# A Hyena block with routed experts on one core: half a forward transform, and work moved between VectorE, ScalarE and GpSimd

## The chip, the cores and the metric

The kernel runs on one core of a Trainium2 chip. The metric is the device time of one execution in microseconds; the median of the runs counts. The engines are TensorE (PE; PEld is its weight load), VectorE (DVE), ScalarE (ACT), GpSimd (POOL) and SyncE (SP, which issues most DMAs). Everything is computed in float32.

## The reference

Eight sequences of 512 tokens with 256 channels pass a long-convolution mixer and a layer of experts, each with a residual and a layer norm without gain (`_layernorm`).

```python
def mixer(x):                                  # x: 8 x 512 x 256
    u = x @ W_in + b_in                        # 768 channels
    uc = short_conv(u, short_w, short_b)       # three taps along the tokens
    x0, x1, v = split(uc, 3)
    v = v * x1
    k = gen_filter(512, ...)                   # 512 x 256, a small net of sines times a decay
    v = causal_fft_conv(v, k, filter_bias)     # product of spectra of length 1024
    return (v * x0) @ W_out + b_out

def ffn(x):                                    # 4096 tokens
    probs = softmax(x @ gate_w.T)              # 16 experts
    top_w, top_idx = top_k(probs, 4)
    top_w = top_w / sum(top_w)
    routed = sum over the 4 of top_w * (silu(x @ w1.T) * (x @ w3.T)) @ w2.T
    shared = (silu(x @ sw1.T) * (x @ sw3.T)) @ sw2.T
    return routed + shared

x = layernorm(x + mixer(x))
x = layernorm(x + ffn(x))
```

## The kernel before

**Mixer, once for each sequence b.** `front` multiplies the transposed input with W_in on TensorE: six products `u_ps` (m = 0 and 1 are the gate x0, 2 and 3 are x1, 4 and 5 are v), 128 channels by 512 tokens each, L409. `convolve_short` does the three taps: ACT writes u + bias and the scaled middle tap (L392, L393), DVE adds the two lagged taps in place (L398). `gated_v` multiplies v by x1. TensorE transposes v in four blocks of 128 tokens (`vt_ps`, L451), ACT evicts (L427), and `transform` (L472) does the forward transform: four outputs (cosine and sine part, two halves of 128 frequencies), each two matmuls of 128x512. ACT evicts each into `vf`. `product` multiplies `vf` with the filter's spectrum on DVE (L488 to L502) into `pf`; `convolved` transforms back (`y_ps`, L522); `gated_y` adds the filter bias and multiplies with the gate x0 on DVE (L538); `normed` multiplies with W_out (`z_ps`, L594). `residual` adds b_out to the input tile `xn` on DVE (L579); `add_z` adds z_ps (L614) and takes the mean and variance with batch-norm statistics on DVE (L554, L555). `scaled` takes the square root on ACT (L562), the reciprocal on DVE and normalizes on ACT (L570) into `x1`. `filter_transform` makes the filter's spectrum once, with the same `transform`.

**Routing.** `turned` transposes x1; `router` computes the gate logits (`l_ps`, L640), picks four experts and their weights on DVE and stores weight and return address beside each token in `x1`. `route` ranks the tokens of each expert with five matmuls (`r_ps`, L780 and L782: one for totals, four with a lag to sum over the four token groups q) and DVE turns ranks into row numbers (`at`). `scatter` sends each token's row four times to the experts' lists `xs` in DRAM, in 16 indirect DMAs on POOL (L925). `shared` computes the shared expert; its sum with x1 goes to DRAM (`kept`).

**Experts.** The sequences form two sets, 0 to 5 and 6 to 7; `listed` makes lists of tiles of 128 rows, 111 tiles for the first set (in three batches) and 47 for the second. `fetch` loads four tiles and DVE picks out each row's weight `sel` and return address `to` (L1061 to L1068). `expert_pair` takes two tiles at a time: transposes (`xr_ps`, L1098), ACT copy, first layer (`h_ps`, L1112), silu on ACT (L1123), product on DVE (L1126), transposes (L1132), ACT copy (L1137), second layer (`o_ps`, L1144), then the eviction with the row weight, on ACT (two halves, L1155) or on DVE (L1157), whichever the planner thinks is free. Two indirect DMAs on POOL (L1166) send the rows back to `results`, by token. `returned` loads the results of a set when its last is sent; `add_up` adds the four of each token (L1199, L1201) with statistics as above, and `finished` normalizes and writes out.

**Order.** All engines are in order, and the order is fixed when the program is built: `Plan` simulates jobs. Each job yields turns (engine, cost, needs, buffers, rank); the planner takes for each engine the lowest rank among those that can start about now. `known` times get a delay of `LATE` = 0.2 us, after TensorE `PE_LATE` = 1 us. Buffers are rings: eight PSUM banks `ps`, six `b2` (128x512) and nine `b4` (128x1024), and small rings such as `sel`.

Of the kernel before, what the change touches and what calls it, by code (L numbers as in the profile page):

```python
# [53 lines left out]
class Plan:  # L54
# [5 lines left out]
    PE_LATE = 1  # L60
# [142 lines left out]
def layer(  # L203
# [56 lines left out]
    plan.ring(h=3, xr=2, sel=3, xrt=2, act=2, actt=2, ob=3, at=4)  # L260
# [45 lines left out]
    fwd_sb = const.tile([P, 2, 2 * NF], F32, name="fwd_sb")  # L306
# [70 lines left out]
    tap_b = const.tile([P, 6], F32, name="tap_b")  # L377

# [3 lines left out]
    def taps_offset():  # L382

        yield turn("DVE", 0.4, ["chan"])
        nc.vector.tensor_tensor(tap_b, chan_sb[:, :, 2], chan_sb[:, :, 3], ALU.mult)
        nc.vector.tensor_tensor(tap_b, tap_b, chan_sb[:, :, 4], ALU.add)
        plan.done("tap_b")

    def convolve_short(b, m, u_ps, h, dst):
        yield turn("ACT", 1.46, [("u", b, m), "tap_b"], ["b2"])  # L390
        u, hu = sb("b2", 0, [P, T], f"u_{b}_{m}")
        nc.scalar.activation(u, u_ps, AF.Identity, bias=chan_sb[:, m, 3:4])  # L392
        nc.scalar.activation(dst, u_ps, AF.Identity, bias=tap_b[:, m : m + 1], scale=chan_sb[:, m, 2:3])  # L393
        plan.let(h)
        plan.done(("u+", b, m))
        yield turn("DVE", 1.5, [("u+", b, m)])
        for lag in (1, 2):
            nc.vector.scalar_tensor_tensor(  # L398
                dst[:, lag:], u[:, : T - lag], chan_sb[:, m, 2 - lag : 3 - lag], dst[:, lag:], ALU.mult, ALU.add
            )  # L400
        plan.let(hu)
        plan.done(("conv", b, m))
# [28 lines left out]
    def front(b):  # L431
        rank = 2 + b * 0.01
        for i in range(KD):
            yield turn("PE", 4 * PASS[T], [("xt", b)], ["ps", "b2", "b4:v"] if i == 0 else ["ps", "b2"])
            if i == 0:
                v, hv = sb("b4:v", 0, [P, KD, T], f"v_{b}")
            cx, hc = sb("b2", 0, [P, T], f"cx_{b}_{i}")
            project(b, KD + i, cx)
            yield turn("PE", 4 * PASS[T], [("xt", b)], ["ps"])
            project(b, 2 * KD + i, v[:, i, :])  # L440
            plan.spawn(gated_v(b, i, v, cx, hc), rank)
        plan.spawn(gates(b), rank + 0.005)
        for q2 in range(QT // 2):
            yield turn("PE", 4 * PASS[P], [("v", b, 0), ("v", b, 1)], ["ps", "b4:vt"] if q2 == 0 else ["ps"])
            if q2 == 0:
                vt, ht = sb("b4:vt", 0, [P, QT, D], f"vt_{b}")
            t_ps, h = ps([P, 2, D], f"vt_ps_{b}_{q2}")
            for j in range(2):
                q = 2 * q2 + j
                for i in range(KD):  # L450
                    nc.tensor.transpose(t_ps[:, j, i * P : (i + 1) * P], v[:, i, q * P : (q + 1) * P], ident)  # L451
            plan.done(("vt_ps", b, q2))
            plan.spawn(evict(vt[:, 2 * q2 : 2 * q2 + 2, :], t_ps, h, 0.6, ("vt", b, q2), ("vt_ps", b, q2)), rank)
        plan.let(hv)
        for part in range(2):
            for m in range(2):
                first = part == m == 0
                needs = [("vt", b, q2) for q2 in range(QT // 2)]
                yield turn("PE", 4 * PASS[T], [*needs, "fwd"], ["ps", "vf"] if first else ["ps"])
                if first:  # L460
                    vf, hf_ = sb("vf", 1, [P, 2, 2, 2, D], f"vf_{b}")
                transform(vf, vt, part, m, b)
        plan.let(ht)
        plan.spawn(product(b, vf, hf_), rank)

    def transform(dst, src, part, m, b):


        v_ps, h = ps([P, 2, D], f"v_ps_{b}_{part}{m}")
        at = part * NF + m * P  # L470
        for k in range(2):
            nc.tensor.matmul(v_ps, lhsT=fwd_sb[:, k, at : at + P], rhs=src[:, k::2, :], start=k == 0, stop=k == 1)  # L472
        plan.done(("vf_ps", b, part, m))
        plan.spawn(evict(dst[:, part, m, :, :], v_ps, h, 0.6, ("vf", b, part, m), ("vf_ps", b, part, m)), 1.9)
# [74 lines left out]
    def stats_of(src, name):  # L549
        tiles["mv", name] = sb("ln", 4, [P, QT, 8], f"mv_{name}")  # L550

    def add_stats(src, q, name):
        mv = tiles["mv", name][0]
        nc.vector.bn_stats(mv[:, q, 2:], src[:, q, :])  # L554
        nc.vector.bn_aggr(mv[:, q, :2], mv[:, q, 2:])  # L555

    def scaled(dst, src, name):
# [3 lines left out]
        rstd = mv[:, :, 2]  # L561
        nc.scalar.activation(rstd, mv[:, :, 1], AF.Sqrt, bias=eps_sb)  # L562
        plan.done(("sd", name))
        yield turn("DVE", 0.4, [("sd", name)])
        nc.vector.reciprocal(rstd, rstd)
        nc.vector.scalar_tensor_tensor(mv[:, :, 3], mv[:, :, 0], -1.0, rstd, ALU.mult, ALU.mult)
        plan.done(("rs", name))
        yield turn("ACT", 4 * 0.39, [("rs", name)])
        for q in range(QT):
            nc.scalar.activation(  # L570
                dst[:, q, :D], src[:, q, :], AF.Identity, bias=mv[:, q, 3:4], scale=mv[:, q, 2:3]
            )
# [3 lines left out]
    def residual(b):  # L576
        yield turn("DVE", 1.25, [("xn", b)])
        xn = xns[b][0]
        nc.vector.tensor_tensor(xn, xn, b_out_sb[:, None, :].to_broadcast([P, QT, D]), ALU.add)  # L579
        plan.done(("xb", b))  # L580

    def normed(b, y, hy):

        rank = 2 + b * 0.01
        for q2 in range(QT // 2):
            yield turn("PE", 8 * PASS[D], [("y", b, 0), ("y", b, 1), ("xn", b), "w_out"], ["ps", "ln"] if q2 == 0 else ["ps"])
            if q2 == 0:
                xn, hx = xns[b]
                stats_of(xn, f"a{b}")
# [14 lines left out]
        yield turn("ACT", 0.0, [("zs", b, 0), ("zs", b, 1)], ["x1"])  # L604
# [7 lines left out]
    def add_z(b, q2, xn, z_ps, h):  # L612
        yield turn("DVE", 0.69 + 1.2, [("z", b, q2), ("xb", b)])
        nc.vector.tensor_add(xn[:, 2 * q2 : 2 * q2 + 2, :], xn[:, 2 * q2 : 2 * q2 + 2, :], z_ps)  # L614
        for q in range(2 * q2, 2 * q2 + 2):
            add_stats(xn, q, f"a{b}")
        plan.let(h)
        plan.done(("zs", b, q2))
# [151 lines left out]
    def route(b):  # L770
# [5 lines left out]
        yield turn("PE", 1.0, [("mask", b), "seg"], ["ps"])  # L776
# [3 lines left out]
        nc.tensor.matmul(r_ps[:, 1], lhsT=tri_sb[:, 1, :], rhs=mask, start=True, stop=True)  # L780
        for lag in range(QT):
            nc.tensor.matmul(  # L782
                r_ps[:, 0, lag:],
                lhsT=tri_sb[:, min(lag, 1), :],
                rhs=mask[:, : QT - lag],
                start=lag == 0,
                stop=lag == QT - 1,
            )
        plan.done(("rank", b))
        yield turn("DVE", 2.1, [("rank", b), "blank", *earlier, *counted], ["at"])  # L790
        row = small([P, QT, NE], "row")
        nc.vector.tensor_tensor(row, r_ps[:, 0], counts[i][:, None, :].to_broadcast([P, QT, NE]), ALU.add)
        tot = small([P, NE], "etot")
        nc.vector.tensor_reduce(tot, r_ps[:, 1].rearrange("p q e -> p e q"), AX.X, ALU.add)
# [8 lines left out]
        nc.vector.tensor_tensor(counts[i], counts[i], tot, ALU.add)  # L803
# [155 lines left out]
    def filter_transform():  # L959
# [29 lines left out]
        for part in range(2):  # L989
            for m in range(2):  # L990
                yield turn("PE", 4 * PASS[T], [("g", 0), ("g", 1), "fwd"], ["ps"])
                transform(gf, decay_sb, part, m, "g")
        yield turn("DVE", 3.2, [("vf", "g", i, m) for i in range(2) for m in range(2)])

        for m in range(2):
            for part in range(2):
                nc.vector.scalar_tensor_tensor(
                    hf[:, part, m, :],
                    gf[:, 1 - part, m, 0, :],
                    sign_sb[:, 1 - part : 2 - part],  # L1000
# [22 lines left out]
    def fetch(f):  # L1023
# [34 lines left out]
        sel, hsel = sb("sel", 3, [P, 4, 2], f"sel_{f}", home=home, uses=2 * len(of))  # L1058
        to, _ = home.tile([P, 4], I32, tag="to", bufs=3, name=f"to_{f}"), None
# [13 lines left out]
    def expert_pair(p, f, xr4, hxr):  # L1073
# [51 lines left out]
        yield turn("DVE", 0.42, [("silu", p)])  # L1125
        nc.vector.tensor_mul(act[:, :n], act[:, :n], h_ps[:, :n, HE:])  # L1126
# [22 lines left out]
        on_act = plan.clock["ACT"] < plan.clock["DVE"]  # L1149
        yield turn("ACT" if on_act else "DVE", 0.78 if on_act else 0.69, [("o_ps", p), ("sel", f)], ["ob"])  # L1150
        sel, to, hsel = tiles["sel", f]
        o, ho = sb("ob", 3, [P, 2, D], f"o_{p}", home=home)
        if on_act:
            for j in range(n):
                nc.scalar.activation(o[:, j], o_ps[:, j], AF.Copy, scale=sel[:, j0 + j, 0:1])  # L1155
        else:
            nc.vector.tensor_tensor(  # L1157
                o[:, :n], o_ps[:, :n], sel[:, j0 : j0 + n, 0:1].to_broadcast([P, n, D]), ALU.mult
            )
# [20 lines left out]
    def returned(i, seqs):  # L1180
        of = [p for p, (k, _, _) in enumerate(pairs) if BATCHES[k][0] == i]
        yield turn("POOL", 0.0, [*(("os", p) for p in of), *(("kept", b) for b in seqs)])
        for b in seqs:
            yield turn("SP", 0.5, (), ["b4:sum", "ln"])
            acc, hacc = sb("b4:sum", 0, [P, QT, D], f"sum_{b}")
            stats_of(acc, f"f{b}")
# [10 lines left out]
    def add_up(b, q, acc, got, h):  # L1197
        yield turn("DVE", 1.54 + 0.6, [("got", b, q), ("sum", b)])
        nc.vector.tensor_tensor(got[:, :2], got[:, :2], got[:, 2:], ALU.add)  # L1199
        for k in range(2):  # L1200
            nc.vector.tensor_tensor(acc[:, q, :], acc[:, q, :], got[:, k, :], ALU.add)  # L1201
        add_stats(acc, q, f"f{b}")
        plan.let(h)
        plan.done(("sum", b, q))

    def finished(b, acc, hacc):
        yield turn("ACT", 0.0, [("sum", b, q) for q in range(QT)])
# [24 lines left out]
def shape_constants():  # L1232
# [8 lines left out]
    fwd = np.concatenate([np.cos(turn), -np.sin(turn)], 1)  # L1241
# [11 lines left out]
    found = {"places": places, "tri": tri, "seg": np.concatenate(seg), "pos": pos, "decay": decay, "fwd": fwd, "inv": fwd.T / CH, "sign": np.stack([even, -even], 1)}  # L1253
# [39 lines left out]
```

## Time and profile before

| | |
|---|---|
| median of 3 runs | 681.0 us (680.23 to 682.18) |
| profiled execution | 681.17 us |
| its span | 679.2 us |
| mean granted TensorE clock | 0.947 |
| busy us: PE / PEld / DVE / ACT / POOL | 597.0 / 436.8 / 463.5 / 336.6 / 321.3 |
| DMA | 116.30 MB, mean 171 GB/s |

The page of a profile shows one execution: busy time of each engine, the span in 40 slices, the DMA queues, the chain of work that ended last, and the costliest groups of instructions with their mean time. Other views of the same trace give stretches of time, single instructions in order, and who waited for whom. Matmuls are pipelined and their ends are modelled, so a row of matmuls is best priced by the start of the next one.

### The profile page before, as it was taken

Reading aid. Unit: us, or ns where it says so; the run is one execution under the profiler, and the core shown is the slowest. Engines: PE = TensorE matmul, PEld = TensorE weight load, DVE = VectorE, ACT = ScalarE, POOL = GpSimd, SP = SyncE. Lnnn points to the kernel's source line nnn. Section 1 sums busy time; section 2 is a strip of 40 time slices with the busy share of each in tenths; the row PEclk is TensorE's granted clock in tenths of the full one; section 3 lists DMA queues with packets and bytes.
Section 4 is the critical chain, followed back from the end, with each engine's and each line's share of the span. In section 5 each row is a group of like instructions: output and inputs, shape, how many; then the busy total and the mean of one; then the engine's idle time right before and its main releaser. Section 6 shows DMA issues by size and latency. Waiting matters only on the chain.

```text
span 679.2 us, 9957 instructions
## 1 busy us (share of the span) xinstructions
PE 597.0 (88%) x2618; PEld 436.8 (64%) x2618; DVE 463.5 (68%) x1164; ACT 336.6 (50%) x654; POOL 321.3 (47%) x580
## 2 busy tenths in 40 slices
PE   6597989989999999999999999899899898888700
PEld 2243647556577677588778777777678786776500
DVE  2768689699896797895797475656222337878745
ACT  2242353634737644837444574273343544967702
POOL 0000003628068178248688518637885764555510
PEclk9798898999999999999999999999899998999955
DMA  8974101514345115335386415327764449899372
GB/s 275 354 244 150 32 1 45 188 48 136 119 136 187 51 67 196 110 118 170 116 272 204 148 52 178 105 91 241 237 207 134 139 137 382 298 410 337 133 288 114
DMA packets 66784, 116.30 MB, mean 171 GB/s; under 512 B 11351, under 2 KB 47781, under 8 KB 66730
## 3 DMA queue, kind: packets, MB, share of 16 engines
q1 hardware_dynamic: 53002, 80.00, 36.2%
q0 software_dynamic: 13728, 35.69, 14.0%
q8 instruction: 22, 0.36, 0.2%
q14 instruction: 32, 0.26, 0.1%
HBM read 62.44 MB, written 57.11 MB: 176 GB/s over the span
## 4 chain that ended last, share of the span: by engine, by line
PE 54%; DVE 17%; POOL 9%; issue 7%; DMA 7%; ACT 3%; SPq 1%; POOLq 0%; ACTq 0%; DVEq 0%
PE h_ps L1112 10%; PE u_ps L409 9%; PE v_ps L472 8%; POOL results L1166 7%; PE y_ps L522 6%; PE o_ps L1144 4%; PE hs_ps L726 3%; PE z_ps L594 3%; DMA got<-results 3%; DMA results<-o,to 2%; PE xr_ps L1098 2%; POOL xs L925 2%; DVE sum L1201 2%; PE os_ps L747 2%; PE l_ps L640 1%
## 5 line engine op out<-in xcount | busy, mean ns | idle before, releaser
L925 POOL DMA_INDIRECT xs<-x,at x128 | 134.7, 1053 | 205.3 <-DVE counts L803 116.5
L1166 POOL DMA_INDIRECT results<-o,to x158 | 163.6, 1036 | 121.1 <-ACT o L1155 61.6
L1112 PE MATMUL h_ps<-w_sb,xrt 128*128 x632 | 151.2, 386 | 1.8 <-ACT xrt L1103 1.7
L1112 PEld LDWEIGHTS h_ps<-w_sb,xrt 128*128 128x128 f32 x632 | 119.6, 193 | 19.8 <-ACT xrt L1103 3.1
L409 PE MATMUL u_ps<-xt,w_in_sb 128*128 128x512 f32 x192 | 92.3, 621 | 3.9 <-DMA xt<-in_x_t 3.9
L1144 PE MATMUL o_ps<-w_sb,actt 128*128 x316 | 82.6, 389 | 9.9 <-ACT actt L1137 9.9
L522 PE MATMUL y_ps<-inv_sb,pf 128*128 128x256 f32 x256 | 67.7, 417 | 11.2 <-DVE pf L502 6.1
L1144 PEld LDWEIGHTS o_ps<-w_sb,actt 128*128 128x128 f32 x316 | 58.6, 193 | 23.9 <-ACT actt L1137 13.5
L1123 ACT ACTIVATE act<-h_ps 128x256 f32<-128x256 f32 (+1 forms) x80 | 30.2, 381 | 82.4 <-PE h_ps L1112 65.8
L1155 ACT ACTIVATE o<-o_ps,sel 128x256 f32<-128x256 f32 x110 | 46.1, 472 | 48.4 <-PE o_ps L1144 38.4
L392 ACT ACTIVATE u<-u_ps,chan_sb 128x512 f32<-128x512 f32 x48 | 33.1, 690 | 70.7 <-PE u_ps L409 29.8
L522 PEld LDWEIGHTS y_ps<-inv_sb,pf 128*128 128x128 f32 x256 | 51.9, 209 | 24.7 <-DVE pf L502 8.6
L409 PEld LDWEIGHTS u_ps<-xt,w_in_sb 128*128 128x128 f32 x192 | 36.9, 200 | 43.3 <-issue 42.4
L1126 DVE TENSOR_TENSOR act<-act,h_ps 128x256 f32<-128x256 f32 (+1 forms) x80 | 32.2, 410 | 44.7 <-ACT act L1123 44.7
L472 PE MATMUL v_ps<-vt,fwd_sb 128*128 128x512 f32 x128 | 57.6, 592 | 0.0
L1103 ACT COPY xrt<-xr_ps 128x512 f32<-128x512 f32 (+1 forms) x80 | 45.3, 589 | 20.2 <-PE xr_ps L1098 18.9
L1098 PE MATMUL xr_ps<-ident,xr 128*128 128x128 f32 x316 | 45.4, 275 | 0.7 <-PE h_ps L1132 0.6
L1098 PEld LDWEIGHTS xr_ps<-ident,xr 128*128 128x128 f32 x316 | 38.0, 142 | 8.1 <-issue 3.6
L472 PEld LDWEIGHTS v_ps<-vt,fwd_sb 128*128 128x128 f32 x128 | 23.6, 190 | 25.4 <-issue 24.9
L1132 PE MATMUL h_ps<-ident,act 128*128 128x128 f32 x158 | 29.9, 279 | 10.1 <-DVE act L1126 9.9
L1137 ACT COPY actt<-h_ps 128x256 f32<-128x256 f32 (+1 forms) x80 | 29.0, 375 | 17.7 <-PE h_ps L1132 16.3
L1132 PEld LDWEIGHTS h_ps<-ident,act 128*128 128x128 f32 x158 | 20.3, 141 | 22.7 <-DVE act L1126 14.6
(146 smaller groups left out, 893.3 us busy)
## 6 DMA issues: line engine op xcount, KB each, us to landing
xr<-xs SPq DMA_DIRECT2D x158, 144.0 KB
got<-results SPq DMA_DIRECT2D x32, 512.0 KB
xs<-blank SPq DMA_DIRECT2D x62, 144.0 KB
w_sb<-in_experts SPq DMA_DIRECT2D x17, 384.0 KB
xt<-in_x_t SPq DMA_DIRECT2D x8, 512.0 KB
xn<-in_x SPq DMA_DIRECT2D x8, 512.0 KB
kept<-acc SPq DMA_DIRECT2D x8, 512.0 KB
sum<-kept SPq DMA_DIRECT2D x8, 512.0 KB
```

The source lines that it names most:

```text
L392: nc.scalar.activation(u, u_ps, AF.Identity, bias=chan_sb[:, m, 3:4])
L409: nc.tensor.matmul(u_ps, lhsT=w_in_sb[:, k, m * P : (m + 1) * P], rhs=xt[:, k, :], start=k == 0, stop=k == KD - 1)
L472: nc.tensor.matmul(v_ps, lhsT=fwd_sb[:, k, at : at + P], rhs=src[:, k::2, :], start=k == 0, stop=k == 1)
L522: nc.tensor.matmul(y_ps[:, c, :], lhsT=pf[:, k // 2, k % 2, c, i * P : (i + 1) * P], rhs=inv_sb[:, k, :], start=k == 0, stop=k == 3,)
L925: move = nc.gpsimd.indirect_dma_start(out=xs[i], out_offset=bass.IndirectOffsetOnAxis(ap=at[:, q, k : k + 1], axis=0), in_=x1[:, q, :], in ...
L1098: nc.tensor.transpose(t_ps[:, j, k, :], xr[:, j, k * P : (k + 1) * P], ident)
L1103: nc.scalar.copy(xrt[:, :n], t_ps[:, :n])
L1112: nc.tensor.matmul(h_ps[:, j, :], lhsT=xrt[:, j, k, :], rhs=w_sb[:, k, bass.ds(at[j], D)], start=k == 0, stop=k == KD - 1,)
L1132: nc.tensor.transpose(a_ps[:, j, :], act[:, j, :], ident)
L1144: nc.tensor.matmul(o_ps[:, j, :], lhsT=actt[:, j, :], rhs=w_sb[:, 2, bass.ds(at[j], D)], start=True, stop=True)
L1155: nc.scalar.activation(o[:, j], o_ps[:, j], AF.Copy, scale=sel[:, j0 + j, 0:1])
L1166: move = nc.gpsimd.indirect_dma_start(out=results[i], out_offset=bass.IndirectOffsetOnAxis(ap=to[:, j0 + j : j0 + j + 1], axis=0), in_=o[: ...
```

## The change

1. **Forward transform.** Tokens are transposed by parity (even tokens first). Only 128 of the 256 frequencies are multiplied, the even and the odd tokens apart (one 128x512 matmul each); the other 128 follow from sum and difference. ACT evicts the even part, DVE adds and subtracts (`joined`), from SBUF and PSUM. The tables and the filter's order follow; `fwd_sb` halves.
2. **Ranks.** Two matmuls; DVE keeps a running count over the four groups.
3. **Gate.** For m = 0 and 1, ACT writes all three scaled taps, POOL adds the lagged ones. The buffer is a `b4` instead of a `b2`.
4. **Residual bias** on POOL.
5. **Norms.** The last add of a row also gives its sum; ACT squares the difference from the mean and sums (`squares`).
6. **Expert weights** are multiplied into the activation, half by half, on DVE; ACT evicts `o_ps` with one plain copy.
7. **Planner.** `PE_LATE` is 0.2; the rings of `sel` and `to` go from 3 to 6 and 8; some costs follow the new work.

```diff
-    PE_LATE = 1
+    PE_LATE = 0.2
...
     def convolve_short(b, m, u_ps, h, dst):
+        if m < KD:
+            yield turn("ACT", 2.15, [("u", b, m), "tap_b"], ["b4:u"])
+            u, hu = sb("b4:u", 0, [P, 2, T], f"u_{b}_{m}")
+            nc.scalar.activation(
+                dst, u_ps, AF.Identity, bias=tap_b[:, m : m + 1], scale=chan_sb[:, m, 2:3]
+            )
+            for k in range(2):
+                nc.scalar.activation(
+                    u[:, k], u_ps, AF.Identity, bias=lag_b[:, m, k : k + 1], scale=chan_sb[:, m, k : k + 1]
+                )
...
+            yield turn("POOL", 2.4, [("u+", b, m)])
+            for lag in (1, 2):
+                nc.gpsimd.tensor_tensor(dst[:, lag:], dst[:, lag:], u[:, 2 - lag, : T - lag], ALU.add)
...
-                    nc.tensor.transpose(t_ps[:, j, i * P : (i + 1) * P], v[:, i, q * P : (q + 1) * P], ident)
+                    at = slice(2 * P * q2 + j, 2 * P * (q2 + 1), 2)
+                    nc.tensor.transpose(t_ps[:, j, i * P : (i + 1) * P], v[:, i, at], ident)
...
-        for k in range(2):
-            nc.tensor.matmul(v_ps, lhsT=fwd_sb[:, k, at : at + P], rhs=src[:, k::2, :], start=k == 0, stop=k == 1)
-        plan.done(("vf_ps", b, part, m))
-        plan.spawn(evict(dst[:, part, m, :, :], v_ps, h, 0.6, ("vf", b, part, m), ("vf_ps", b, part, m)), 1.9)
+    def half_transform(src, part, k, b):
+        v_ps, h = ps([P, 2, D], f"v_ps_{b}_{part}{k}")
+        at = fwd_sb[:, k, part * P : (part + 1) * P]
+        nc.tensor.matmul(v_ps, lhsT=at, rhs=src[:, k::2, :], start=True, stop=True)
+        if k:
+            plan.done(("half", b, part, 1))
+            return v_ps, h
+        even, he = sb("b2", 0, [P, 2, D], f"even_{b}_{part}")
+        plan.done(("even", b, part))
+        plan.spawn(evict(even, v_ps, h, 0.6, ("half", b, part, 0), ("even", b, part)), 1.9)
+        return even, he
+
+    def joined(dst, part, halves, b):
+        yield turn("DVE", 2 * 0.69, [("half", b, part, k) for k in range(2)])
+        (even, h0), (odd, h1) = halves
+        nc.vector.tensor_tensor(dst[:, part, 0], even, odd, ALU.add)
+        if part:
+            even, odd = odd, even
+        nc.vector.tensor_tensor(dst[:, part, 1], even, odd, ALU.subtract)
...
-        nc.vector.bn_stats(mv[:, q, 2:], src[:, q, :])
-        nc.vector.bn_aggr(mv[:, q, :2], mv[:, q, 2:])
+    def add_up_to(dst, src, q, name):
+        mv = tiles["mv", name][0]
+        nc.vector.scalar_tensor_tensor(
+            dst[:, q, :], src, 1.0, dst[:, q, :], ALU.mult, ALU.add, accum_out=mv[:, 0, q : q + 1]
+        )
...
+        nc.vector.tensor_scalar(mv[:, 1, qs], mv[:, 0, qs], -1.0 / D, None, ALU.mult)
...
+        for q in qs:
+            nc.scalar.activation(
+                unused, src[:, q, :], AF.Square, bias=mv[:, 1, q : q + 1], accum_out=mv[:, 2, q : q + 1]
+            )
...
-        nc.vector.tensor_tensor(xn, xn, b_out_sb[:, None, :].to_broadcast([P, QT, D]), ALU.add)
+        nc.gpsimd.tensor_tensor(xn, xn, b_out_sb[:, None, :].to_broadcast([P, QT, D]), ALU.add)
...
-        nc.tensor.matmul(r_ps[:, 1], lhsT=tri_sb[:, 1, :], rhs=mask, start=True, stop=True)
-        for lag in range(QT):
-            nc.tensor.matmul(
-                r_ps[:, 0, lag:],
-                lhsT=tri_sb[:, min(lag, 1), :],
-                rhs=mask[:, : QT - lag],
...
+        for k in range(2):
+            nc.tensor.matmul(r_ps[:, k], lhsT=tri_sb[:, k, :], rhs=mask, start=True, stop=True)
...
+        nc.vector.tensor_copy(before[:, 0], counts[i])
+        for q in range(QT):
+            after = before[:, q + 1] if q + 1 < QT else counts[i]
+            nc.vector.tensor_tensor(after, before[:, q], r_ps[:, 1, q], ALU.add)
+        nc.vector.tensor_tensor(row, r_ps[:, 0], before, ALU.add)
...
-        nc.vector.tensor_mul(act[:, :n], act[:, :n], h_ps[:, :n, HE:])
+        for j in range(n):
+            nc.vector.scalar_tensor_tensor(
+                act[:, j], h_ps[:, j, HE:], sel[:, j0 + j, 0:1], act[:, j], ALU.mult, ALU.mult
+            )
...
-            for j in range(n):
-                nc.scalar.activation(o[:, j], o_ps[:, j], AF.Copy, scale=sel[:, j0 + j, 0:1])
-        else:
-            nc.vector.tensor_tensor(
-                o[:, :n], o_ps[:, :n], sel[:, j0 : j0 + n, 0:1].to_broadcast([P, n, D]), ALU.mult
-            )
+        nc.scalar.copy(o[:, :n], o_ps[:, :n])
```

## Prediction

> **What bounds the kernel now.** I read the page's busy line first, then the busy time by stage (stretches cut at places that the chain names), then the chain of waits, then single rows for prices. The profiled execution took 681.2 us, of which 679.2 are span; the median of the runs shown is 681.0, so a sum made against the profiled time needs no correction.
>
> ```profile
> PE 597.0 (88%) x2618; PEld 436.8 (64%) x2618; DVE 463.5 (68%) x1164; ACT 336.6 (50%) x654; POOL 321.3 (47%) x580
> ```
>
> TensorE is the busiest, but a share over the span mixes five stages. Columns below: stage, its length, then busy time and instruction count of PE, its weight loads, DVE, ACT and POOL, then the granted clock, the DMA engines' share and GB/s.
>
> ```profile
> 0.00:110.00 110.00, 89.22 (x256) 49.67 (x257) 74.61 (x140) 39.26 (x61) 1.35 (x9) 0.89 0.50 163
> 110.00:453.00 343.00, 337.44 (x1497) 244.61 (x1496) 263.51 (x670) 182.84 (x338) 198.21 (x345) 1.00 0.41 134
> 453.00:556.00 103.00, 95.62 (x505) 81.73 (x504) 39.14 (x126) 46.06 (x112) 72.37 (x138) 0.98 0.54 174
> 556.00:641.00 85.00, 72.58 (x358) 59.70 (x357) 66.41 (x177) 58.87 (x125) 43.19 (x78) 0.96 0.88 325
> 641.00:680.00 39.00, 2.16 (x7) 1.11 (x7) 19.84 (x55) 9.58 (x20) 6.21 (x11) 0.56 0.47 175
> ```
>
> Call them A to E. B, half of the time, is TensorE's: 337 of 343 us at full clock. A is a start-up chain. In C, POOL is nearly full too: half of its 138 instructions are one-element memsets, the other 69 indirect DMAs follow each other in 1.28 us (470.43, 471.69 and 472.96 below), so 88 of 103 us. D has a busy DMA (0.88) and TensorE at 85%. E has no matmul: the last results come back, are added up and normalized.
>
> ```profile
> 470.43 0.96 POOL xs L925
> 471.69 0.96 POOL xs L925
> 472.96 0.96 POOL xs L925
> 474.22 0.99 POOL results L1166
> 475.51 0.99 POOL results L1166
> ```
>
> **TensorE's part.** The chain gives the old forward transform of one sequence its own price, and the timeline the five old rank matmuls (each matmul written in the kernel shows as two records):
>
> ```profile
> 271.74 6.87 PE v_ps L472 x16
> 455.95 0.33 PE L780 MATMUL r_ps<-mask,tri_sb 128*128 128x64 f32 x2
> 456.12 1.02 PE L782 MATMUL r_ps<-mask,tri_sb 128*128 128x64 f32 x8
> 456.98 0.68 PE L726 MATMUL hs_ps<-x1t,w_sb 128*128 128x512 f32 x1
> ```
>
> Half of 6.87 goes nine times (eight sequences and the filter): 30.9 us. The ranks take 1.03 us (455.95 to 456.98, the next matmul) for ten records; four remain, so 0.62 x 8 = 5.0 us. Together 36 us. Nothing is added to TensorE; the transposes read v with a stride of two elements, taken at the old 0.14 to 0.15 us each (doubled, 64 of them would cost 9).
>
> Where it goes: I add up the matmul rows (0.86 us for 512 columns, 0.43 for 256, 0.15 for a transpose) along TensorE's order in both programs. The last sequence's gate logits (l_ps, 450.0 us in the trace) stand behind 419 us of matmul work before and 375 after. That is 44 earlier: the 36, and 8 us of expert tiles that now come behind. Of the 44, 11.6 lie in A (three halves and two ranks), 32.6 in B.
>
> **The other engines, per sequence.**
> - DVE loses the gate's four lag steps (2 x 0.747 + 2 x 0.750 = 2.99), the residual bias (1.22) and, behind the output projection, 2 x 0.673 + 4 x (0.411 + 0.182) = 3.72. It gains four joins of halves (0.69 each, the 128x512 row with one PSUM input: 2.76), four adds that also sum (1.92 by the 0.481 row of a 128x256 scalar_tensor_tensor, L997), two tiny steps (0.36), and 0.46 for running counts in the ranks. Net -2.4. The sum's output may cost a further small operation: nothing to 0.18 (the batch-norm aggregate's row) each, so -2.4 to -1.7.
> - ACT: the gate needs six passes at 0.78 in place of four (2 x 0.78 + 2 x 0.69): +1.74; two evictions of 0.584 go (-1.17); four squares at 0.59 (the 128x256 row L570), each waiting for the one in front, nothing to 0.3 more: +2.4 to +3.6. Net +2.9 to +4.1.
> - POOL: four adds over 511 columns, one over 1024. No row shows such an add here. Lower ends: DVE's rows, 0.685 for 512 and 1.22 for 1024. Upper ends: twice the identity's affine select per element (128 columns in 0.286, so 2.23 ns), for two inputs: 2.3 and 4.6. I take that select's rate once, 1.14 and 2.29, since it is POOL's own read-and-write row: 6.9 us per sequence (4.0 to 13.8).
>
> The experts: 158 products with the weight at 128x128 (0.288) replace 80 wide ones (32.2 us): +13.3 on DVE; the 24 scaled evictions on DVE (16.5) go. On ACT 110 scaled halves (51.9) become 79 copies of 0.594 (46.9). The `to` buffers, for which DVE waited 18.1 us, go from 3 to 8.
>
> **Stage by stage.** A: -11.6 of matmul; but a join stands between the last half and the product (1.38 in place of a 0.58 eviction), for the filter and the two first sequences: +2.4. So -9.2 (-11.6 to -5).
>
> B: -32.6 if TensorE stays as full. Does the cover hold? DVE: 263.5 less some 13 over 310 us, 81% (77% before). ACT: 183 + 25, 67% (53%). POOL: up to the last sequence's scatter 168 DMAs x 1.28, 24 gate adds and 5 biases x my prices: 254 of 310, 82% (172 DMAs, 220 of 343, 64% before). In C, with POOL at 86%, TensorE idles 7.2%; in B 1.6%. On the line between the two, 82% gives 6.2%, 14 us more idle time. But the tiles' results and the scatters, which rank first on POOL, are what others wait for, and the gate is wanted only after two transforms; I take half, +7 (0 to +14). Queued behind a late gate add are scatters, and on DVE, behind the gating that waits for it, the products and expert steps. B: -25.6.
>
> C: 8 us of expert tiles more, and POOL has 70 DMAs instead of 66 from the last sequence's first scatter to the first set's last result (+5): +7 (0 to +12).
>
> D: ACT gets 23 squares (13.6 us) on 58.9 of 85, as full as TensorE then; DVE loses about 7 (0.2 to 0.4 per added-up tile row, its six scaled evictions, against +3.6). DMA is as before. +1 (-4 to +10). E: DVE's eight add-ups become shorter by 2.5 in all; the last one now passes to ACT for a square (0.59 and a handoff) in place of 0.61 of statistics: -1 (-3 to +3).
>
> The planner's delay behind matmuls falls from 1.0 to 0.2, so its order leaves less slack at handoffs; the trace shows ACT's silu starting 0.04 us after the modelled end of h_ps (449.14, 449.18). I price that at nothing; its risk is inside B's and D's bounds.
>
> Sum: -9.2 - 25.6 + 7 + 1 - 1 = -27.8, so 653 us. The steps' bounds, added in quadrature, give 640 to 666 for this case alone.
>
> **A rule against the change.** Before, POOL reads no tile in SBUF for arithmetic, and DVE's two-input rows are steady (fa 1.224, pf 1.219 and 1.226 us); no row shows what happens beside a POOL add. The Trainium skill's "SBUF — State Buffer", section "Who interferes with whom", says that a VectorE instruction with two SBUF inputs contends with a GpSimd instruction that reads SBUF, and that the loser blocks fully. Were each of the 40 adds to hold up VectorE for its whole length, VectorE would lose 55 us, most of it in B, and the sum would stand near or above the time before; without the rule it stays at 653. Another page, "VectorE: DVE Perf Modes", section "Two Vector instructions with no wait between them", counts an operation that also writes its accumulator as two instructions; no row here shows one.
>
> **Rivals.**
> 1. TensorE's 36 us come through whole, and the freed `to` waits add a little: 643 us. For it: B's cover of 98% with DVE at 77%. Against: every other engine's share rises in B. 25%.
> 2. POOL and DVE become B's joint limit: the full 14 us of idle time, and, should the two engines get in each other's way, 29 POOL adds in B that each cost DVE one operation of about 1 us, making it 90% full, 8 more. B gives 10.6 instead of 25.6: 668 us. 15%.
> 3. Slower: the GpSimd queue becomes the bound between the first scatter and the first set's last result. Before, 306 us of DMA issue fill 445 us there (110.8 to 556); with the 24 gate adds and 5 biases at my prices it is 344, so about 100 us of slack remain. It decides when a 511-column add takes over some 4.0 us (24 x 2.9 + 5 x 5.8 = 99). At 4.6 us the queue is 20 us late, a total of 700. Against it: twice the affine select is only 2.3. 10%.
>
> The forecast keeps 50%.
>
> **How the numbers follow.** 638 to 674 takes in the forecast's own range and most of rivals 1 and 2; what is left out is rival 3 and the far side of rival 1. About 0.3% (2 us) is what a measurement of this kernel can tell from no change. Faster: 0.50 + 0.25 + nearly all of 0.15 = 0.88; same 0.02; slower 0.10.
>
> **What would show it.** Right: v_ps of a sequence at 3.44 us; l_ps of the last sequence near 415 us; B's TensorE share 94 to 97%; POOL adds near 1.1 and 2.3 us; DVE busy 430 to 440, ACT near 370, POOL busy near 376. Wrong: l_ps of the last sequence above 430 (B lost more), DVE's pf rows stretched beyond 1.3 us (rival 2), POOL never idle before the second set (rival 3), D longer than 95 us with ACT full (my +1 failed).

## The result, and the profile after

The changed kernel takes 689.65 us (median of 4 runs, 688.29 to 692.38), the kernel before 680.69 beside it: a ratio of 1.0133, interval 1.0098 to 1.0168. It is slower; the forecast was 653. The profiled execution took 692.38 us, 2.7 above the median; its span is 690.6.

The page's busy line after (columns as before the change):

```profile
PE 573.6 (83%) x2498; PEld 423.5 (61%) x2498; DVE 462.2 (67%) x1239; ACT 366.9 (53%) x747; POOL 376.2 (54%) x620
```

TensorE lost 23 us, and ACT and POOL are where the sum had them. VectorE should have been at 430 to 440 and is at 462, as much as before. The same five stages, cut where their work now ends:

```profile
0.00:110.00 110.00, 85.72 (x259) 50.20 (x260) 88.79 (x162) 45.39 (x78) 27.15 (x29) 0.89 0.50 166
110.00:460.00 350.00, 313.01 (x1325) 225.22 (x1323) 259.38 (x672) 185.09 (x352) 221.13 (x354) 0.94 0.37 126
460.00:563.00 103.00, 98.90 (x521) 84.29 (x521) 39.81 (x156) 52.59 (x115) 74.35 (x143) 0.98 0.57 181
563.00:650.00 87.00, 75.97 (x398) 63.84 (x396) 55.73 (x191) 68.09 (x162) 45.21 (x83) 1.00 0.89 316
650.00:691.00 41.00, 0.00 (x0) 0.00 (x0) 18.46 (x61) 15.70 (x44) 8.40 (x15) 0.50 0.48 181
```

B is the stage that went wrong: 7 us longer instead of 25.6 shorter, with TensorE idle for 37 of its 350 us (5.6 of 343 before). Cut at one landmark, the gate logits l_ps, the difference of the spans (+11.4) falls apart like this (us; starts of l_ps from its tile view):

| | first l_ps | first to last | last l_ps to the end |
|---|---|---|---|
| before | 94.4 | 355.5 | 229.4 |
| after | 85.8 | 373.2 | 231.6 |
| difference | -8.5 | +17.7 | +2.2 |

The groups of instructions of the changed kernel show VectorE's loss row by row (line, engine, operation, out<-in, count; busy us and mean ns; idle time before and its releaser):

```profile
L419 DVE SCALAR_TENSOR_TENSOR v<-u,chan_sb,v 128x511 f32<-128x511 f32 x16 | 17.3, 1083 | 4.9 <-ACT v L414 4.8
L442 DVE TENSOR_TENSOR v<-v,cx 128x512 f32<-128x512 f32 x16 | 13.8, 865 | 0.1
L753 DVE TENSOR_TENSOR nth<-nth,mask 128x64 f32<-128x64 f32 x8 | 4.9, 607 | 0.3
L407 POOL TENSOR_TENSOR x<-x,u 128x511 f32<-128x511 f32 x16 | 22.1, 1382 | 47.6 <-ACT u L400 47.5
L639 POOL TENSOR_TENSOR xn<-xn,b_out_sb 128x1024 f32<-128x1024 f32 x8 | 19.3, 2416 | 28.0 <-DMA xn<-in_x 28.0
```

The same VectorE rows in the kernel before:

```profile
L398 DVE SCALAR_TENSOR_TENSOR v<-u,chan_sb,v 128x511 f32<-128x511 f32 x16 | 11.9, 742 | 2.8 <-ACT v L393 2.8
L421 DVE TENSOR_TENSOR v<-v,cx 128x512 f32<-128x512 f32 x16 | 11.0, 685 | 0.1
L694 DVE TENSOR_TENSOR nth<-nth,mask 128x64 f32<-128x64 f32 x8 | 1.8, 229 | 0.3
```

A lag step of v was 0.742 us and is 1.083. The timeline of the changed kernel (start, duration) shows one such place, VectorE first, then GpSimd:

```profile
124.36 1.40 DVE L730 TENSOR_SCALAR mask<-taken 128x64 f32<-128x64 f32 x1
...
129.36 2.26 DVE L753 TENSOR_TENSOR nth<-nth,mask 128x64 f32<-128x64 f32 x1
131.66 0.25 DVE L754 TENSOR_SCALAR x<-nth,places_sb 128x64 f32<-128x64 f32 x1
```

```profile
124.42 4.83 POOL L407 TENSOR_TENSOR x<-x,u 128x511 f32<-128x511 f32 x4
129.21 2.33 POOL L639 TENSOR_TENSOR xn<-xn,b_out_sb 128x1024 f32<-128x1024 f32 x1
```

The nth step works on 64 columns and took 0.23 us before; here it starts 0.15 us behind GpSimd's bias add and ends 0.08 us behind it. It stands on the chain that ended last.

### The profile page after: what moved, and what is told of

The parts are those of the page before. It is cut to its first block, busy times and chain, and to the rows that moved or that the text cites. A ratio compares the mean times of both kernels' runs of the same rounds, so it can differ in the third digit from the quotient of the medians.

```text
span 690.6 us, 10031 instructions
## 1 busy us (share of the span) xinstructions
PE 573.6 (83%) x2498; PEld 423.5 (61%) x2498; DVE 462.2 (67%) x1239; ACT 366.9 (53%) x747; POOL 376.2 (54%) x620
## 4 chain that ended last, share of the span: by engine, by line
PE 43%; DVE 30%; ACT 9%; DMA 6%; issue 6%; SPq 5%; POOL 1%; ACTq 0%; DVEq 0%; POOLq 0%
PE h_ps L1169 12%; PE o_ps L1205 5%; PE y_ps L563 5%; PE u_ps L430 4%; PE z_ps L654 3%; DMA got<-results 3%; PE xr_ps L1155 3%; DVE v L419 2%; PE v_ps L496 2%; DVE pf L530 2%; DVE pf L531 2%; DVE fa L529 2%; PE hs_ps L785 2%; PE os_ps L806 2%; SPq L962 2%
## 5 line engine op out<-in xcount | busy, mean ns | idle before, releaser
L979 POOL DMA_INDIRECT xs<-x,at x128 | 130.9, 1023 | 109.4 <-issue 94.6
L1169 PE MATMUL h_ps<-w_sb,xrt 128*128 x632 | 152.9, 388 | 3.2 <-ACT xrt L1160 3.1
L1185 DVE SCALAR_TENSOR_TENSOR act<-h_ps,sel,act 128x128 f32<-128x128 f32 x158 | 47.4, 344 | 83.4 <-ACT act L1180 83.4
L563 PE MATMUL y_ps<-inv_sb,pf 128*128 128x256 f32 x256 | 74.6, 445 | 28.6 <-DVE pf L543 12.4
L563 PEld LDWEIGHTS y_ps<-inv_sb,pf 128*128 128x128 f32 x256 | 54.9, 224 | 46.3 <-DVE pf L543 17.7
L407 POOL TENSOR_TENSOR x<-x,u 128x511 f32<-128x511 f32 (+1 forms) x32 | 42.3, 1327 | 48.9 <-ACT u L400 47.5
L1180 ACT ACTIVATE act<-h_ps 128x256 f32<-128x256 f32 (+1 forms) x80 | 30.5, 383 | 71.5 <-PE h_ps L1169 70.0
L1212 ACT COPY o<-o_ps 128x512 f32<-128x512 f32 (+1 forms) x80 | 45.7, 579 | 25.2 <-PE o_ps L1205 23.9
L413 ACT ACTIVATE u<-u_ps,chan_sb 128x512 f32<-128x512 f32 x32 | 22.2, 695 | 54.3 <-DVE cx L419 22.0
L419 DVE SCALAR_TENSOR_TENSOR v<-u,chan_sb,v 128x511 f32<-128x511 f32 (+1 forms) x32 | 33.6, 1051 | 5.4 <-ACT v L414 4.8
L639 POOL TENSOR_TENSOR xn<-xn,b_out_sb 128x1024 f32<-128x1024 f32 x8 | 19.3, 2416 | 28.0 <-DMA xn<-in_x 28.0
```

The lines of the kernel that those rows point to most:

```text
L407: nc.gpsimd.tensor_tensor(dst[:, lag:], dst[:, lag:], u[:, 2 - lag, : T - lag], ALU.add)
L419: nc.vector.scalar_tensor_tensor(dst[:, lag:], u[:, : T - lag], chan_sb[:, m, 2 - lag : 3 - lag], dst[:, lag:], ALU.mult, ALU.add)
L563: nc.tensor.matmul(y_ps[:, c, :], lhsT=pf[:, k // 2, k % 2, c, i * P : (i + 1) * P], rhs=inv_sb[:, k, :], start=k == 0, stop=k == 3,)
L979: move = nc.gpsimd.indirect_dma_start(out=xs[i], out_offset=bass.IndirectOffsetOnAxis(ap=at[:, q, k : k + 1], axis=0), in_=x1[:, q, :], in ...
L1169: nc.tensor.matmul(h_ps[:, j, :], lhsT=xrt[:, j, k, :], rhs=w_sb[:, k, bass.ds(at[j], D)], start=k == 0, stop=k == KD - 1,)
L1185: nc.vector.scalar_tensor_tensor(act[:, j], h_ps[:, j, HE:], sel[:, j0 + j, 0:1], act[:, j], ALU.mult, ALU.mult)
```

## The experiments

The theory after the result: the 40 GpSimd adds hold VectorE while they read SBUF. Rivals: GpSimd's own time is the cost (the queue is late); the new order of the planner is (short delay, other rings); VectorE's joins are.

One of the sets of kernels ran on a chip that ran the kernel before in 735.8 us; its four kernels were run again where the kernel before took 680 to 681, and only those numbers are used here. In the profiles from the first chip VectorE stands idle for 42 to 61 us in which it waits for nothing that the profile shows; on the others it is 1 us or less.

### GpSimd's adds: their reading, their time, or the order?

**The adds given back to VectorE**, nothing else:

```diff
-        if m < KD:          # gate: three scaled taps on ACT, adds on POOL
-            ...
-        nc.gpsimd.tensor_tensor(xn, xn, b_out_sb..., ALU.add)
+        nc.vector.tensor_tensor(xn, xn, b_out_sb..., ALU.add)
```

> The changed kernel with the gate's convolution and the residual bias back as before (lagged taps and bias on VectorE, two ScalarE passes per gate half), everything else as changed, and the order planned anew. Theories port and queue: 655 to 672 us, since VectorE gets 34 us of work back but is held up by nothing. Theory order: 680 to 690 us.

669.26 us, ratio 0.9829 (0.9790 to 0.9869). Moving these adds to GpSimd costs 20 us; but the planner made another order here.

**The order kept, the adds cut to one column:**

```diff
-  nc.gpsimd.tensor_tensor(dst[:, lag:], dst[:, lag:], u[:, 2 - lag, : T - lag], ALU.add)
+  nc.gpsimd.tensor_tensor(dst[:, lag : lag + 1], dst[:, lag : lag + 1], u[:, 2 - lag, :1], ALU.add)
-  nc.gpsimd.tensor_tensor(xn, xn, b_out_sb..., ALU.add)
+  nc.gpsimd.tensor_tensor(xn[:, 0, :1], xn[:, 0, :1], b_out_sb[:, :1], ALU.add)
```

> The changed kernel in its own order on every engine, but each GpSimd add covers one column instead of 511, 510 or 1024, so most of the gate's lagged taps and of the residual bias is left out. If the adds cost the time, by whatever way (rival theories port and queue), it comes to 650 to 668 us, and VectorE's lag steps are back at 0.75 us. If the loss lies in the new order and in the joins between the halves (theory order), it stays at 680 to 690 us.

664.36 us, ratio 0.9771 (0.9742 to 0.9799): 25.3 us less than the change, with every instruction in the same order. The short adds still take 12 us of GpSimd's time.

**The order kept, the adds turned into memsets**, which keep GpSimd busy but read nothing:

```diff
-  nc.gpsimd.tensor_tensor(dst[:, lag:], ..., ALU.add)
+  nc.gpsimd.memset(dst[:, lag:], 1.0)
+  nc.gpsimd.memset(dst[:, lag:], 1.0)
-  nc.gpsimd.tensor_tensor(xn, ..., ALU.add)
+  nc.gpsimd.memset(xn, 1.0)
+  nc.gpsimd.memset(xn, 0.5)
```

> The changed kernel in its own order, but each GpSimd add is two memsets of the same region: about the same GpSimd time (1.0 to 1.3 us for 511 columns), writes alone and no read of SBUF; the gate's lagged taps and the input behind the residual are left out. Theory port (a GpSimd instruction that reads SBUF holds VectorE's two-input instructions): VectorE's lag steps return from 0.74 to 1.08 us to 0.75, and the time falls to 655 to 672 us. Theory queue (GpSimd's own time delays scatters and gates): it stays at 683 to 692 us.

667.94 us, ratio 0.9810 (0.9782 to 0.9838). The page's busy lines of the two, one column first:

```profile
PE 562.6 (85%) x2498; PEld 417.0 (63%) x2498; DVE 432.9 (65%) x1239; ACT 367.5 (56%) x747; POOL 326.4 (49%) x620
```

```profile
PE 567.4 (85%) x2498; PEld 419.4 (63%) x2498; DVE 434.9 (65%) x1239; ACT 366.6 (55%) x747; POOL 364.7 (55%) x660
```

VectorE has the same 1239 instructions in all three: 432.9, 434.9 and, with the adds, 462.2 us. Against the one-column kernel, 49 us of memsets (their groups added up) cost 3.6 us of time and hold VectorE for 2; 62 us of adds hold it for 29 and cost 25. Of the 29 us between the profiled spans of the changed kernel and the one-column kernel, 11 are TensorE's own busy time (573.6 against 562.6, the same 2498 records) at a mean granted clock of 0.921 against 0.941: TensorE waits longer, and its matmuls take longer too. The groups of the memset kernel put the rows beside those shown above:

```profile
L420 DVE SCALAR_TENSOR_TENSOR v<-u,chan_sb,v 128x511 f32<-128x511 f32 x16 | 11.9, 742 | 3.6 <-ACT v L415 3.6
L443 DVE TENSOR_TENSOR v<-v,cx 128x512 f32<-128x512 f32 x16 | 11.0, 684 | 0.1
...
L407 POOL MEMSET x<- 128x511 f32 x16 | 8.6, 536 | 34.0 <-ACT x L396 33.9
```

So it is not GpSimd's time as such, and not the order. That it is the adds' reading fits VectorE's rows: v's steps, with two inputs in SBUF, are stretched, while `y` (L579), with one input in PSUM, takes 1.111 us in the changed kernel and 1.110 in the one-column kernel, although four of its 16 lie beside GpSimd adds. It is not shown alone: a memset is also a shorter instruction (0.53 us for 511 columns, the add 1.38), and one that reads without adding was not tried.

**The adds alone, on the kernel before**, with ACT's third pass for each gate half, which they need:

```diff
+        if m < KD:
+            ...
+            for lag in (1, 2):
+                nc.gpsimd.tensor_tensor(dst[:, lag:], dst[:, lag:], u[:, 2 - lag, : T - lag], ALU.add)
...
-        nc.vector.tensor_tensor(xn, xn, b_out_sb..., ALU.add)
+        nc.gpsimd.tensor_tensor(xn, xn, b_out_sb..., ALU.add)
```

> The kernel before with the gate's lagged adds and the residual bias on GpSimd alone. Theory port: VectorE's two-input rows stretch by 20 to 30 us in all, and the time is 685 to 702 us. Theory that the adds hurt only together with the new order: 665 to 680 us.

705.09 us, ratio 1.0375 (1.0331 to 1.0419). Its groups:

```profile
L419 DVE SCALAR_TENSOR_TENSOR v<-u,chan_sb,v 128x511 f32<-128x511 f32 x16 | 16.9, 1059 | 8.7 <-ACT v L414 8.6
L442 DVE TENSOR_TENSOR v<-v,cx 128x512 f32<-128x512 f32 x16 | 15.0, 936 | 0.3
```

The same rows are stretched by similar amounts, without any other part of the change; VectorE's rows that stand in both kernels take 34 us longer in all, beside 63 us of adds. The kernel is 25 us slower although VectorE was relieved of 34 us of its own steps. The order is new here as well, so these 25 us are not the adds' price alone, and not the same measure as the 25 of the one-column kernel.

### The rest of the change

**The short delay taken back**, in the changed kernel:

```diff
-    PE_LATE = 0.2
+    PE_LATE = 1
```

> The changed kernel with the planner's delay behind matmuls at 1.0 as before, everything else as changed. Theory order: a good part of the loss goes, 665 to 678 us. Theories port and queue: 685 to 692 us, as GpSimd still adds the same tiles beside the same VectorE work.

693.17 us, ratio 1.0180 (1.0156 to 1.0204): 3.5 us behind the change. The delay is not what made it slow.

**Halved transform and short ranks alone**, the delay left at 1, and then with it at 0.2; and **the delay alone** (the second line, on the kernel before):

```diff
+    def half_transform(src, part, k, b): ...      # parts 1 and 2 of the change as they are
+    def joined(dst, part, halves, b): ...
...
-    PE_LATE = 1
+    PE_LATE = 0.2
```

> The kernel before with the halved forward transform and the two rank matmuls alone (planner's delay 1.0), on a chip that runs the kernel before in 680 us. If TensorE's work sets the time of the long stage: 648 to 656 us. If VectorE's chain sets it (theory VectorE: the joins are 25 us of work more for it): 666 to 680 us.

> As the kernel with the halved transform and ranks alone, but the planner's delay behind matmuls 0.2. On the slower chip this order was 3% faster than the one with 1.0. If that holds here: 8 to 20 us faster than with 1.0. If it was the chip's slower instruction supply: within 4 us.

> The kernel before with the planner's delay behind matmuls at 0.2 and nothing else. Theory delay: the short delay is a gain of its own, whatever TensorE's work: 660 to 672 us. Theory pair: it pays only where TensorE has less to do than VectorE, as with the halved transform: 677 to 684 us.

Halves at 1: 679.6 us, ratio 0.9988 (0.9964 to 1.0012). Halves at 0.2: **657.9 us, ratio 0.9660 (0.9629 to 0.9691)**, the best version here; it beats both kernels. The delay alone: 681.88, ratio 1.0022 (0.9999 to 1.0044). Each alone is worth nothing, the two together 22 us. Where the halves' gain goes at the long delay is in TensorE's waits (all rows of that view added up): 47.2 us before, 72.2 with the halves at 1, 50.9 at 0.2. TensorE's busy time fell by some 28 us, its waits rose by 25; the short delay takes 21 of them away again. Some rows, halves at 1 first (who waits, for whom; us in all, times, longest):

```profile
PE h_ps L1152 <- DVE act L1146: 17.1, 15, 3.5
PE y_ps L544 <- DVE pf L524: 11.4, 8, 4.5
PE g_ps L999 <- issue: 8.0, 1, 8.0
```

```profile
PE y_ps L544 <- DVE pf L524: 14.8, 9, 6.2
PE h_ps L1152 <- DVE act L1146: 10.3, 10, 2.1
```

Of the 21, six are gaps in stage A in which TensorE waits for nothing that the profile shows ("issue": 8.0 and 2.0 in all); seven are waits of the experts' transposes for VectorE's product. But the gap alone explains no gain: with the delay alone, the kernel before loses its gap too (6.9 us, then 0.3), and its time stays.

**The same pair in the full change without GpSimd's adds:** the first experiment's kernel at `PE_LATE = 1`.

> The change with gate adds and bias on VectorE and PE_LATE 1 in place of 0.2. Its twin at 0.2 ran in 669.3 us. If the short delay and the halving pay only together whatever else is in the kernel, as in the pair without the other parts (679.6 at 1, 657.9 at 0.2), 685 to 693. If the delay matters only where the weights are put on behind the experts, 667 to 673.

684.92 us, ratio 1.0056 (1.0040 to 1.0073), against 669.26 at 0.2. TensorE's waits: 71.5 and 56.7 us. The pair pays only together here too.

**Every join done twice**, in the best version:

```diff
         nc.vector.tensor_tensor(dst[:, part, 0], even, odd, ALU.add)
+        nc.vector.tensor_tensor(dst[:, part, 0], even, odd, ALU.add)
...
         nc.vector.tensor_tensor(dst[:, part, 1], even, odd, ALU.subtract)
+        nc.vector.tensor_tensor(dst[:, part, 1], even, odd, ALU.subtract)
```

> The kernel with the halved transform, the short ranks and the delay of 0.2 (657.9 us), each add and subtract of a join issued twice, order unchanged: 24.5 us of VectorE work more, 21.8 of it for the eight sequences. Theory VectorE (its chain bounds the sequences' stage): 672 to 682 us. If TensorE still bounds that stage: 658 to 664 us.

679.0 us, ratio 0.9968 (0.9950 to 0.9985): 36 more joins of 0.68 us, 24.5 us of VectorE work, cost 21 us. One "issue" gap of 7.5 us (1.7 in the best version) is in that, so the joins themselves cost some 15: more than half of their length is on the path.

**One kind of GpSimd add at a time**, in the best version: the bias alone, then the gate's alone.

```diff
-        nc.vector.tensor_tensor(xn, xn, b_out_sb..., ALU.add)      # first kernel
+        nc.gpsimd.tensor_tensor(xn, xn, b_out_sb..., ALU.add)
...
+        if m < KD: ... nc.gpsimd.tensor_tensor(dst[:, lag:], ...)  # second kernel
```

> The kernel with the halved transform, the short ranks and the delay of 0.2 (657.9 us), with the residual bias alone on GpSimd (eight adds, 19 us). Theory port: each add holds up about its own length of VectorE's work less the 1.22 us it gives away: 660 to 668 us. Without contention VectorE is relieved of 10 us: 648 to 656 us.

> As that kernel, but the gate's lagged adds on GpSimd and the bias on VectorE: 32 adds, 42 us, VectorE relieved of 24. Theory port: 668 to 684 us, most of the loss of both. Without contention: 642 to 655 us.

669.06 us, ratio 0.9813 (0.9779 to 0.9847), and 683.35, ratio 1.0028 (1.0006 to 1.0051): 11 and 25 us over 657.9. Eight bias adds of 2.4 us and 32 gate adds of 1.3 us each spoil the version, the gate's by all it had gained. VectorE's rows that stand in both kernels take 12 and 16 us longer, beside 20 and 45 us of adds. With the gate's adds VectorE is busy for less than in the best version (485.7 against 492.5 us), yet TensorE's waits go from 50.9 to 68.4: VectorE's load alone does not explain the loss. The order is new in both, and its part was not separated.

**The batch-norm statistics back on VectorE**, in the first experiment's kernel; and **the ring sizes alone**, in the best version:

```diff
-        nc.vector.scalar_tensor_tensor(..., accum_out=...)         # and the squares on ACT
+        nc.vector.bn_stats(mv[:, q, 2:], src[:, q, :])
+        nc.vector.bn_aggr(mv[:, q, :2], mv[:, q, 2:])
...
-        sel, hsel = sb("sel", 3, ...)                              # second kernel; `to`: 3 to 8
+        sel, hsel = sb("sel", 6, ...)
```

> The changed kernel with the lagged adds and the bias back on VectorE (669.3 us), and the norms' statistics back on VectorE as well. If the squares relieve VectorE where it bounds: 673 to 682 us, slower than 669. If ScalarE's squares cost as much by handoffs and by filling ScalarE in the last stage: 663 to 670 us.

> The kernel with the halved transform, the short ranks and PE_LATE 0.2 (657.9 us), with only the ring sizes of the change added (sel 6, to 8), the selection weights still put on behind the experts. It separates the rings from the weights in the 8 us by which the change's version with VectorE's adds and VectorE's statistics (665.8 us) stands above 657.9. If the rings do it (tiles are released in another order), 664 to 667; if the weights put on the activations do it, 656 to 660.

665.83 us, ratio 0.9785 (0.9761 to 0.9810), and 661.59, ratio 0.9727 (0.9692 to 0.9763). Between 657.9 and the 669.3 of the full change without GpSimd's adds lie, as a ladder: rings +3.7, weights on the activations +4.2, squares on ACT +3.4. Each rung also has another order, and the intervals of neighbours touch or nearly do; no gain was seen from any of the three. The rungs for rings and weights lie between what was expected for either, so that question is not decided.

Five of the results lie a little outside the range expected by the theory that they are nearest to: 705.09, 693.17, 669.06 and 684.92 us by 3.1, 1.2, 1.1 and 0.1, and the 21.7 us between 679.6 and 657.9, for which 8 to 20 were expected.

## Why the prediction was wrong

**The step that failed most: the GpSimd adds, priced as if beside VectorE.** The sum gave them 6.9 us per sequence on GpSimd and, through GpSimd's share of B, "+7 (0 to +14)". Their price is on VectorE: 29 us held, 25 us of time, against +7. The paragraph on the rule had the mechanism and worked out a loss near the time before; "no row shows what happens beside a POOL add" was true, and the forecast then kept the case without it. The Trainium skill's "SBUF — State Buffer", section "Who interferes with whom", says that the loser blocks fully, and that a GpSimd instruction that only writes doesn't contend with two inputs of VectorE; the runs agree for the nth step, which ended with the bias add, and for the memsets. The size lies between: 29 us held of the 62 us that GpSimd's adds take. The adds also held a step with one SBUF input (the mask step, 1.40 us where the one-column kernel has 0.20).

**The second: B's -32.6.** With the adds cut to one column, first to last l_ps is 352.6 us, against 355.5 before: a gain of 3. The stretch from the first to the last l_ps before, with one column, and after (columns as for the stages):

```profile
94.35:449.84 355.49, 346.88 (x1536) 252.50 (x1535) 276.39 (x706) 184.49 (x341) 196.44 (x342) 0.99 0.39 129
77.33:429.91 352.58, 324.55 (x1403) 235.75 (x1401) 262.39 (x738) 192.64 (x366) 191.29 (x361) 0.96 0.38 127
85.83:459.02 373.19, 333.02 (x1403) 240.19 (x1401) 281.32 (x738) 192.65 (x366) 226.15 (x361) 0.94 0.36 120
```

With one column TensorE is busy for 22.3 us less, not 32.6, and idle for 28.0 us where it was 8.6: 19.4 more, not 7. "If TensorE stays as full" failed, and so did a price: the forecast counted the matmuls that go and kept the old times for those that stay. The granted clock in the stretch is 0.96 in place of 0.99, and y_ps, with the same 256 records, is busy for 76.2 us in place of 67.7 (these over the whole span). Most of the new idle time is waits for the products. The waits view, before, one column, after:

```profile
PE y_ps L522 <- DVE pf L502: 6.1, 4, 2.6
...
PE y_ps L522 <- DVE pf L490: 2.0, 1, 2.0
```

```profile
PE y_ps L563 <- DVE pf L543: 11.7, 10, 2.2
PE y_ps L563 <- DVE pf L531: 10.6, 4, 5.7
```

```profile
PE y_ps L563 <- DVE pf L543: 12.4, 10, 2.2
PE y_ps L563 <- DVE pf L531: 10.8, 4, 4.3
```

8.1, 22.3 and 23.2 us. The step took idle time from how full GpSimd would be; what is late next is VectorE's chain of joins and products between the two transforms, for which the sum had a price (+2.4) in A only. Here this is read from the waits; that the joins are on the path is shown by their doubling in the best version. VectorE need not be full for that: it was busy for 245 of the 330 us from 110 to 440 in the one-column kernel.

So B's miss of 43 us (17.7 against -25.6) is 20.6 of GpSimd's adds (373.2 less 352.6; 12.1 of it idle time of TensorE, 8.5 longer matmuls), 12.4 of idle time beyond the +7, and 10.3 of matmul time that did not fall.

**A:** -8.5 against -9.2, right by two errors. The one-column kernel has its first l_ps at 77.3, 17 us earlier than before: the 6.9 us "issue" gap that the kernel before has in A is nearly gone (1.1 left), which was not foreseen, and the adds gave 8.5 us back.

**C to E:** +2.2 together against +7, inside the bounds. **"I price that at nothing":** the planner's delay alone is worth nothing (681.88), but the halves are worth nothing without it. The sum took the order for neutral.

**Small prices.** A half transform is 3.43 us, as taken. GpSimd's adds are 1.33 and 2.42 us (taken 1.14 and 2.29). The transposes with a stride of two were taken at the old price, but their weight load is 0.207 us, 0.141 before. On VectorE the sum's output is an instruction of its own, as the Trainium skill's "VectorE: DVE Perf Modes", section "Two Vector instructions with no wait between them", counts it; the price is 0.08 us. On ACT the rows show one too, at 0.19:

```profile
L473 PEld LDWEIGHTS vt_ps<-ident,v 128*128 128x128 f32 x64 | 9.3, 207 | 10.7 <-DVE v L442 9.6 <-issue 0.9
...
L613 ACT ACTIVATION_READ_ACCUMULATOR unused<-sum,mv_f 128x1 f32 x32 | 6.2, 192 | 0.0
...
L599 DVE DVE_READ_ACCUMULATOR xn<-z_ps,xn 128x1 f32 x32 | 2.6, 82 | 0.0
```

**Rivals.** The third (GpSimd's queue) is refuted by the memsets: GpSimd was nearly as full (364.7 us against 376.2), and the time only 3.6 us above the one-column kernel. The second had the right mechanism and a size of 8 us where 25 was due; it also carried 14 us of idle time, near the 19.4 that the one-column kernel has, but for a full GpSimd. Its own sign failed: the pf rows have means of 1.285 and 1.276 us, not beyond 1.3, since most of the holds fell on other rows.

**What stays open:** why the halves and the short delay pay only together. That TensorE's waits carry the difference is shown; why the planner's order at the long delay makes them, and what the "issue" gaps of 7 to 8 us are, is not. Nor is it shown why the granted clock is lower in the kernels with more waits. Whether the holding goes by ports, banks or arbitration was not tried.

## What to carry to other kernels

Work that reads SBUF is not free on GpSimd because GpSimd is idle: ask which VectorE instructions it will lie beside, and charge some half of its length there (16 of 45 to 12 of 20 us in the kernels here) until a run says otherwise. When a matmul is replaced by a smaller one and a VectorE step, look at who waits for the product behind it, not at TensorE's share. When the order is planned, test a saving together with the planner's delays: here each alone was worth nothing, and both together 3.4%.

## What the runs showed that was not expected

GpSimd's adds, 62 us of them, hold VectorE for 29 us, small steps of 64 columns among them (0.23 to 2.26 us); its memsets, 49 us, hold it for 2. ACT's accumulator read is 0.19 us behind each square, 12.2 us in all; VectorE's is 0.08. Reading a transpose's operand with a stride of two makes its weight load 0.207 us instead of 0.141.
